# A graph network on one core: parts of edge groups may end in mid-chunk, and gathered rows come in bursts of three chunks

## The chip, the cores and the metric

The kernel runs on 1 core of one Trainium2 chip. The metric is the device time of one execution in microseconds (us). The engines are TensorE (PE, with its weight loads as PEld), VectorE (DVE), ScalarE (ACT), GpSimd (POOL) and SyncE (SP). Each has one stream of instructions, which it works off in the order in which they were written.

## What is computed

There are N = 6250 nodes with 256 features and E = 100,000 edges. The edges are sorted by their target `dst`, and the targets lie denser at low node numbers. Two layers of a graph network sum the rows of the neighbours, each followed by two dense products; at the end come the residual and a layer norm.

```python
def _gin_agg(h, src, dst, eps, n_nodes):
    agg = jax.ops.segment_sum(h[src], dst, num_segments=n_nodes)
    return (1.0 + eps) * h + agg
...
h = _gin_agg(x, src, dst, eps1, n)          # 6250 x 256
h = relu(relu(h @ W1a + b1a) @ W1b + b1b)   # 6250 x 512
h = _gin_agg(h, src, dst, eps2, n)
out = relu(h @ W2a + b2a) @ W2b + b2b       # 6250 x 256
x = _layernorm(x + out)
```

## The kernel before, in words

**Chunks.** The edges are cut into 782 chunks of 128. The first 308 chunks belong to eight crowded tiles of 128 nodes (the "heavy" tiles; seven and 288 chunks in layer 2). Their sums are made by counting edges per pair of nodes and multiplying with whole rows (lines 1734 and 1766 count, 1630 multiplies in layer 1, 1522 in layer 2). All other chunks, 474 in layer 1 and 494 in layer 2, are gathered: for each, GpSimd issues one indirect DMA (line 501) that brings the 128 source rows into SBUF, 256 floats wide in layer 1, 512 in layer 2.

**Groups and parts.** `places` (line 141) packs consecutive chunks into groups of 4h chunks (80 groups; h is 1 to 4). Group by group, the chunks are split into four parts of h chunks. A part may touch at most 32 consecutive nodes, a group at most 128. For each chunk VectorE builds a 128x32 selection matrix (line 1076), and TensorE multiplies it with the gathered rows (line 1127): part b adds into partitions 32b to 32b+31 of a PSUM bank. `members` takes the chunks of a group so that the part changes from one to the next; four chunks in a row thus write to four different strips of 32 partitions. A matmul of float32 shows as two records in the trace.

**Merging.** When the sums of a group are done, ScalarE and VectorE split them in two halves of precision (lines 1157 and 1162), TensorE puts the four parts to their place with two matmuls of a 128x128 matrix `to` (line 1172), and VectorE adds the result into the accumulators of the 1 to 3 node tiles that the group touches (line 1184). In layer 1 two groups share a bank and one turn of splits. When a tile has all its sums, its dense work follows: transposes (line 1234), the first product (line 1273), the second (line 1302); layer 1 writes its rows `h1` to DRAM, which layer 2 gathers.

**Rings.** Gathered rows come in pieces of at most `BURST` = 4 chunks of one group, into a ring of `PIECES` = 6 places. The first gather into a place waits until the sums of the piece that lay there before are done (line 507). Layer 1 sums one piece at a time, layer 2 joins three (`JOIN`).

**What sets the order.** While the program is built, `Plan` (line 293) plays the engines with costs and waits, and writes each engine's instructions in the order that comes out; sums have the first turn on TensorE, merges the second, dense work the third, the products of line 1522 the last. `GATHERS` (us per gather), `LANDINGS` (us until its rows are there), `SUMS` and `TURN` (cost of a piece's matmuls) are such costs. They are not in the program: on the chip an engine takes its stream in this order and waits where data is not there yet. Line 1196 writes matmuls without use where the plan finds TensorE idle late in a layer. The groups are worked off from the highest nodes to the lowest.

Of the kernel before, what the change touches and what calls it, by code (L numbers as in the profile page):

```python
# [17 lines left out]
P = 128  # L18
# [4 lines left out]
BURST = 4  # L23
PIECES = 6
# [116 lines left out]
def places(N, E, c, chunks):  # L141
# [47 lines left out]
GATHERS = (1.28, 1.265)  # L189
LANDINGS = (14.0, 10.0)  # L190
LOAD = 6.0
LANDED = 2.5
SUMS = 0.0021
# [9 lines left out]
BEGAN = 4.5  # L203
# [165 lines left out]
def tile_gin_residual_layernorm(  # L369
# [56 lines left out]
    groups, lo, hi = (a + b for a, b in zip(places(N, E, NC2, NC), places(N, E, NC, NCH)))  # L426
# [4 lines left out]
    NCP = groups[-1][0] + PARTS * groups[-1][1]  # L431
# [43 lines left out]
    members = {}  # L475
# [17 lines left out]
    def gather(number, i, table, width, *places):  # L493

        if i >= len(pieces[number]):
# [9 lines left out]
            for j, (c, b) in enumerate(pieces[number][i][1])  # L505
# [30 lines left out]
    with tc.tile_pool(name="prep", bufs=1) as prep, tc.tile_pool(  # L536
# [10 lines left out]
        assert all(c >= halves * HALF for i in range(EARLY) for c, _ in pieces[1][i][1])  # L547
# [35 lines left out]
        nc.vector.memset(first[0:1, :], 1.0)  # L583
        ones = prep.tile([P, 1], F16, name="ones")
# [32 lines left out]
        for (c, h), top in zip(groups, hi):  # L617
            tops[c : c + PARTS * h] = [top * P + P - 1] * (PARTS * h)
# [80 lines left out]
        def in_groups(g0, g1):  # L699

            c, h = groups[g0]
            return dstf[:, c : c + PARTS * h * (g1 - g0)]

        for g0, g1 in runs:
            h = groups[g0][1]
            nc.tensor.matmul(
                heads[:, PARTS * g0 : PARTS * g1], first,
                in_groups(g0, g1).rearrange("p (g h) -> p g h", h=h)[:, :, 0],
                start=True, stop=True,
            )  # L710
# [12 lines left out]
        compare, add_compare = nc.vector.tensor_tensor, nc.vector.scalar_tensor_tensor  # L723
# [24 lines left out]
        spans = []  # L748
        for g0, g1 in runs:
            c, h = groups[g0]  # L750
            if c + PARTS * h * (g1 - g0) > real:
                g1 -= 1
                spans.append((g1, g1 + 1, (real - groups[g1][0]) // h))
                assert groups[g1][0] + spans[-1][2] * h == real
            if g0 < g1:
                spans.insert(0, (g0, g1, PARTS))

        def beside(do, v, each):

            for g0, g1, parts in spans:  # L760
                c, h = groups[g0]
                n = (PARTS * (g1 - g0 - 1) + parts) * h
                if each:
                    l, f = h, heads[:, PARTS * g0 : PARTS * (g1 - 1) + parts]
                else:
                    l, f = parts * h, bases[:, g0:g1]
                to, of = (
                    a[:, o : o + n].rearrange("p (g l) -> p g l", l=l)
                    for a, o in ((v, c - NC2), (dstf, c))
                )  # L770
                do(to, f.unsqueeze(2).to_broadcast(list(to.shape)), of)

        for each, n in ((True, SLOTS), (False, P)):
            violated(
                lambda v: beside(lambda to, f, d: compare(to, f, d, op=ALU.is_gt), v, each), ng
            )
            violated(
                lambda v: beside(
                    lambda to, f, d: add_compare(
                        to, f, float(n - 1), d, op0=ALU.add, op1=ALU.is_lt  # L780
                    ), v, each,
                ), ng,
            )
# [85 lines left out]
    def ordered(ctx):  # L869
# [13 lines left out]
        def layer(number, ctx, table, width, scale, wa, ba, wb, bias, wide):  # L883
# [177 lines left out]
            def selecting():  # L1061
                for g in order:
# [8 lines left out]
                    sel_token = yield ("get", sel_one if h == 1 else sel_many, 0)  # L1071
# [24 lines left out]
            def sums():  # L1096
# [9 lines left out]
                while i < len(pieces[number]):  # L1106
# [10 lines left out]
                    for i in some:  # L1117
# [7 lines left out]
                        for l, (c, b) in enumerate(pieces[number][i][1]):  # L1125
                            part = [c_ for c_, b_ in members[g] if b_ == b]
                            mm = nc.tensor.matmul(  # L1127
                                pm[b * SLOTS : (b + 1) * SLOTS],
                                sel[:, c - groups[g][0], :], rows_[:, l, :],
                                start=(c == part[0]), stop=(c == part[-1]),  # L1130
                            )
                            if l == 0:
                                together(mm, reads[1:])
                        last_sum[i] = mm
                        fetch_rows(i + PIECES)
                        if i == last[g]:
                            sel_token.used()
                            if g == gs[-1]:
                                plan.then(plan.start, merge([
                                    (k, sels[k][1], SLOTS * len({b for _, b in members[k]}),  # L1140
# [930 lines left out]
```

## Time and profile before

| | us |
|---|---|
| median of three runs (lowest, highest) | 1298.17 (1293.37, 1298.98) |
| the profiled execution | 1295.27 |
| its span, first to last instruction | 1293.5 |
| TensorE busy | 1177.7 (91%) |
| VectorE busy | 876.3 (68%) |
| GpSimd busy (gathers) | 940.9 (73%) |
| ScalarE busy | 555.6 (43%) |

Busy time of GpSimd leaves out the 0.3 us between two gathers that the profile calls "issue". Ends of matmuls are modelled and overlap with the next start, so a cost on TensorE is best read from one start to the next.

### The profile page before, as it was taken

Reading aid. Unit: us, or ns where it says so; the run is one execution under the profiler, and the core shown is the slowest. Engines: PE = TensorE matmul, PEld = TensorE weight load, DVE = VectorE, ACT = ScalarE, POOL = GpSimd, SP = SyncE. Lnnn points to the kernel's source line nnn. Section 1 sums busy time; section 2 is a strip of 40 time slices with the busy share of each in tenths; the row PEclk is TensorE's granted clock in tenths of the full one; section 3 lists DMA queues with packets and bytes.
Section 4 is the critical chain, followed back from the end, with each engine's and each line's share of the span. In section 5 each row is a group of like instructions: output and inputs, shape, how many; then the busy total and the mean of one; then the engine's idle time right before and its main releaser. Section 6 shows DMA issues by size and latency. Waiting matters only on the chain. (4 is left out here: it accounts for less than half of the span.)

```text
span 1293.5 us, 18734 instructions
## 1 busy us (share of the span) xinstructions
PE 1177.7 (91%) x6088; PEld 747.2 (58%) x6088; DVE 876.3 (68%) x2098; ACT 555.6 (43%) x1014; POOL 940.9 (73%) x995
## 2 busy tenths in 40 slices
PE   5689999898998788889888999999999999999987
PEld 3335555554545444554455666767676667776755
DVE  8899889687898898442247867886566656554433
ACT  6335653664245521562454534343343434432221
POOL 7777777777777777777176777777777777777771
PEclk7789999999999999899988999999999999999999
DMA  6755685569546774588299879888898889877782
GB/s 188 216 153 174 213 236 157 186 204 251 153 136 211 194 207 131 163 233 248 79 354 319 284 232 310 266 271 269 288 300 268 288 286 291 290 236 229 236 254 82
DMA packets 190146, 293.86 MB, mean 227 GB/s; under 512 B 67246, under 2 KB 122948, under 8 KB 190040
## 3 DMA queue, kind: packets, MB, share of 16 engines
q0 software_dynamic: 62272, 191.69, 48.0%
q1 hardware_dynamic: 120292, 87.28, 22.4%
q10 hardware_dynamic: 7476, 13.60, 2.9%
q8 instruction: 52, 0.85, 0.3%
q14 instruction: 54, 0.44, 0.1%
HBM read 266.46 MB, written 26.02 MB: 226 GB/s over the span
## 5 line engine op out<-in xcount | busy, mean ns | idle before, releaser
L501 POOL DMA_INDIRECT early<-in_x_dram,srcs x474 | 465.6, 982 | 146.4 <-issue 119.7
L501 POOL DMA_INDIRECT early<-h,srcs x250 | 238.9, 956 | 103.5 <-issue 62.5
L501 POOL DMA_INDIRECT late<-h,srcs x244 | 234.0, 959 | 76.5 <-issue 60.6
L1184 DVE SCALAR_TENSOR_TENSOR acc<-bank,mask,acc 128x512 f32<-128x512 f32 (+1 forms) x374 | 215.6, 608 | 36.9 <-PE bank L1172 35.1
L1127 PE MATMUL bank<-early,sel 128*32 128x256 f32 (+1 forms) x1448 | 140.6, 479 | 52.0 <-DMA early<-in_x_dram,srcs 30.1
L1302 PE MATMUL bank<-wide_w,ht 128*128 128x512 f32 (+1 forms) x392 | 185.4, 597 | 1.6 <-ACT acc L1009 1.5
L1273 PE MATMUL bank<-zt,wide_w 128*128 128x256 f32 (+2 forms) x832 | 180.8, 371 | 3.0 <-ACT zt L1246 3.0
L1273 PEld LDWEIGHTS bank<-zt,wide_w 128*128 128x128 f32 x832 | 150.8, 192 | 33.6 <-ACT zt L1246 5.7
L1522 PE MATMUL bank<-upper,cf 128*128 128x512 f32 (+1 forms) x343 | 152.2, 444 | 5.1 <-ACT upper L1414 4.5
L1522 PE MATMUL bank<-xr,cf 128*128 128x512 f32 (+1 forms) x343 | 138.3, 403 | 2.0 <-DVE xr L1419 2.0
L1076 DVE TENSOR_TENSOR sel<-iota,slot 128x256 f32<-128x256 f32 (+3 forms) x112 | 49.8, 444 | 103.2 <-PE bank L1127 99.2
L1127 PEld LDWEIGHTS bank<-early,sel 128*32 128x32 f32 x1448 | 35.3, 111 | 144.2 <-issue 107.3
L1630 PE MATMUL bank<-xh,cf 128*128 128x512 f32 x392 | 111.9, 428 | 0.3 <-DVE xh L1586 0.3
L1766 DVE TENSOR_TENSOR at<-bank,at 128x490 f32 (+3 forms) x175 | 105.7, 604 | 6.5 <-DVE cb L1696 1.6
L1172 PE MATMUL bank<-split,to 128*128 128x512 f32 (+2 forms) x316 | 89.4, 395 | 21.0 <-DVE split L1162 11.5
L1302 PEld LDWEIGHTS bank<-wide_w,ht 128*128 128x128 f32 (+1 forms) x392 | 69.8, 189 | 62.5 <-issue 55.1
L1302 PE MATMUL bank<-narrow_w,ht 128*128 128x256 f32 (+1 forms) x392 | 102.4, 388 | 2.5 <-ACT ht L1283 2.5
L1157 ACT CAST split<-bank 128x512 fp32r<-128x512 f32 (+2 forms) x121 | 68.8, 577 | 81.7 <-PE bank L1127 77.3
L1162 DVE TENSOR_TENSOR split<-bank,split 128x512 fp32r<-128x512 f32 (+2 forms) x121 | 79.1, 673 | 36.2 <-ACT split L1157 35.7
L1273 PE MATMUL bank<-zt,narrow_w 128*128 128x256 f32 (+2 forms) x432 | 99.2, 375 | 2.3 <-ACT zt L1246 1.6
L1449 ACT CAST cf<-ci 128x512 fp32r<-128x512 uint8 (+3 forms) x91 | 53.7, 592 | 106.7 <-PE bank L1522 86.3
L1696 DVE TENSOR_SCALAR cb<-numbers,spot 128x492 f16<-128x492 f16 (+6 forms) x308 | 85.9, 322 | 19.6 <-PE bank L1734 19.6
(139 smaller groups left out, 1605.7 us busy)
## 6 DMA issues: line engine op xcount, KB each, us to landing
raw<-in_x_dram SPq DMA_DIRECT2D x48, 512.0 KB
h<-h1r ACTq DMA_DIRECT2D x48, 256.0 KB
xr<-h SPq DMA_DIRECT2D x12, 1024.0 KB
acc<-h SPq DMA_DIRECT2D x19, 512.0 KB
early<-in_x_dram,srcs POOLq DMA_INDIRECT x474
r<-in_x_dram SPq DMA_DIRECT2D x22, 256.0 KB
out_dram<-r SPq DMA_DIRECT2D x22, 256.0 KB
acc<-in_x_dram SPq DMA_DIRECT2D x21, 256.0 KB
```

The source lines that it names most:

```text
L501: nc.gpsimd.indirect_dma_start(out=rows_[:, j, :], out_offset=None, in_=table, in_offset=bass.IndirectOffsetOnAxis(ap=srcs[:, c : c + 1], ...
L1127: mm = nc.tensor.matmul(pm[b * SLOTS : (b + 1) * SLOTS], sel[:, c - groups[g][0], :], rows_[:, l, :], start=(c == part[0]), stop=(c == par ...
L1157: nc.scalar.copy(split[:used, 0, i * width : j * width], ap[:used, i * width : j * width])
L1162: nc.vector.tensor_tensor(split[:used, 1, i * width : j * width], ap[:used, i * width : j * width], split[:used, 0, i * width : j * width] ...
L1172: nc.tensor.matmul(pu[:, i * width : (i + 1) * width], to[:used], split[:used, l, i * width : (i + 1) * width], start=(l == 0), stop=(l == 1),
L1184: nc.vector.scalar_tensor_tensor(acc[t], pu[:, i * width : (i + 1) * width], mask[:, t - lo[g], g : g + 1], acc[t], op0=ALU.mult, op1=ALU.add,
L1273: nc.tensor.matmul(ph[:, (f - o) * TILES * P : (f - o) * TILES * P + nb], wa[:, k, f * P : (f + 1) * P], zt[:, k, :nb], start=(k == 0), st ...
L1302: nc.tensor.matmul(po[:m], ht[:, f, i * P : i * P + m], wb[:, f, :], start=(f == 0), stop=(f == KH - 1),)
L1522: nc.tensor.matmul(bank[token.number][:, :width], cf[:m, j, :], of[:m, j, :], start=(j == 0 and of is upper), stop=(j == len(ks) - 1 and o ...
L1630: nc.tensor.matmul(bank[tokens[i].number][:, : 2 * width], cf[:m, j, :], xh[:m, j, :, :].rearrange("p a d -> p (a d)"), start=(k == 0), st ...
L1696: made = nc.vector.tensor_scalar(token.tile[:, :e], numbers[:, :e], spot[:, c : c + 1], None, op0=ALU.is_equal,)
L1766: nc.vector.tensor_tensor(to, bank[token[0].number][:, : NT * w].rearrange("p (k w) -> p k w", w=w), to, op=ALU.add,)
```

## The change

A part may now be a whole number of half chunks long. `places` takes groups of 2 chunks more or less instead of 4 for the 474 chunks beyond the heavy tiles, so h may be 1.5, 2.5 or 3.5. The code gives 60 groups instead of 80 (58 instead of 78 in layer 1): 29 with h = 1.5, 14 with 2.5, 7 with 3.5, 6 with 2, and four others. In the 50 groups with a half, two chunks lie across a border between parts. Each such chunk gets two matmuls with 64 rows, the lower half into one part, the upper half into the next. `BURST` becomes 3 and `PIECES` 8; a piece still ends with its group, so 474 chunks make 172 pieces (before 119), 494 make 180 (before 124), some of them with 1 or 2 chunks. A group with h = 2.5 has pieces of 3, 3, 3 and 1 chunks. The plan's costs change: `LANDINGS` from 14 and 10 to 20 and 12, `SUMS` from 0.0021 to 0.0019, two others by little. Before the layers, the check of the group borders is rewritten and has a few instructions more.

```diff
-BURST = 4
-PIECES = 6
+BURST = 3
+PIECES = 8
...
-            n -= PARTS
-        groups.append((c, n // PARTS))
+            n -= step
+        if n % PARTS and c + n > chunks:
+            n -= n % PARTS
+        groups.append((c, n / PARTS if n % PARTS else n // PARTS))
...
-GATHERS = (1.28, 1.265)
-LANDINGS = (14.0, 10.0)
+GATHERS = (1.285, 1.265)
+LANDINGS = (20.0, 12.0)
...
-SUMS = 0.0021
+SUMS = 0.0019
...
-BEGAN = 4.5
+BEGAN = 5.3
...
+        a + b for a, b in zip(places(N, E, NC2, NC, PARTS), places(N, E, NC, NCH, PARTS // 2))
...
-        members[g] = [
-            (c0 + b * h + i, b) for i in range(h) for b in range(PARTS) if c0 + b * h + i < NCH
-        ]
+        n, l = int(PARTS * h), int(2 * h)
+        ks = sorted(range(n), key=lambda k: (2 * k % l, 2 * k // l))
+        members[g] = [c0 + k for k in ks if c0 + k < NCH]
+        for k in range(n):
+            b, last = 2 * k // l, (2 * k + 1) // l
+            parts_of[c0 + k] = [(b, 0, P)] if b == last else [(b, 0, P // 2), (last, P // 2, P)]
...
-                    sel_token = yield ("get", sel_one if h == 1 else sel_many, 0)
+                    sel_token = yield ("get", sel_one if n <= 2 * PARTS else sel_many, 0)
...
-                        for l, (c, b) in enumerate(pieces[number][i][1]):
-                            part = [c_ for c_, b_ in members[g] if b_ == b]
+                        for k, (l, c, b, p0, p1) in enumerate(some_):
+                            part = [c_ for c_, b_, _, _ in seen if b_ == b]
                             mm = nc.tensor.matmul(
                                 pm[b * SLOTS : (b + 1) * SLOTS],
-                                sel[:, c - groups[g][0], :], rows_[:, l, :],
+                                sel[p0:p1, c - groups[g][0], :], rows_[p0:p1, l, :],
                                 start=(c == part[0]), stop=(c == part[-1]),
                             )
```

In the order of the whole program, the sums' matmuls go from 474 to 574 in layer 1 and from 494 to 594 in layer 2. The merges' go from 156 to 116 and from 160 to 120, VectorE's additions of line 1184 from 186 to 149 and from 188 to 151, the splits on ScalarE and VectorE from 121 to 91 each. The gathers stay 474 and 494. The matmuls without use go from 55 to 35. New line numbers: sums 1149, merges 1194, transposes 1256, first products 1295, second 1324, products with whole rows 1544.

The first place is TensorE's stream in the middle of layer 1, before:

```order
L1127 MATMUL bank_480<-early,sel 32x256 x4
L1734 LDWEIGHTS ca
L1734 MATMUL bank_477<-cb,ca 128x343
L1734 LDWEIGHTS ca
L1734 MATMUL bank_473<-cb,ca 128x343
L1273 MATMUL bank_479<-zt,narrow_w 128x256 x4
L1734 LDWEIGHTS ca
L1734 MATMUL bank_474<-cb,ca 128x343
L1734 LDWEIGHTS ca
L1734 MATMUL bank_477<-cb,ca 128x343
L1302 MATMUL bank_475<-wide_w,ht 128x512 x2
L1127 MATMUL bank_480<-early,sel 32x256 x4
```

and now, in a group with h = 2.5:

```order
L1149 MATMUL bank_491<-early,sel 32x256 x3
L1324 MATMUL bank_493<-wide_w,ht 128x512 x2
L1324 MATMUL bank_496<-wide_w,ht 128x512 x2
L1149 MATMUL bank_491<-early,sel 32x256 x4
L1756 LDWEIGHTS ca
L1756 MATMUL bank_490<-cb,ca 128x441
L1756 LDWEIGHTS ca
L1756 MATMUL bank_490<-cb,ca 128x441
L1149 MATMUL bank_491<-early,sel 32x256 x2
L1652 MATMUL bank_495<-xh,cf 128x512 x4
```

A piece was four matmuls. Now the pieces of this group have 3, 3, 4 and 2: the last two hold the two cut chunks, of which each has two matmuls of 64 rows, and other work stands between the pieces as before.

The second place is TensorE's stream from the last sums of layer 1 on (1302 and 1324 are second products), before:

```order
L1127 MATMUL bank_474<-early,sel 32x256 x4
L1302 MATMUL bank_476<-wide_w,ht 128x512 x2
L1172 MATMUL bank_475<-split,to 128x256 x2
L1302 MATMUL bank_476<-wide_w,ht 128x512 x2
L1234 MATMUL bank_478<-ident,acc 128x128 x2
L1234 MATMUL bank_477<-ident,acc 128x128 x2
L1196 LDWEIGHTS numbers
L1196 MATMUL bank_480<-numbers 128x492
L1273 MATMUL bank_479<-zt,narrow_w 128x128 x4
L1273 MATMUL bank_473<-zt,narrow_w 128x128 x4
L1273 MATMUL bank_474<-zt,narrow_w 128x128 x4
L1273 MATMUL bank_475<-zt,narrow_w 128x128 x4
```

and now:

```order
L1149 MATMUL bank_496<-early,sel 32x256 x4
L1324 MATMUL bank_497<-wide_w,ht 128x512 x2
L1194 MATMUL bank_491<-split,to 128x256 x2
L1295 MATMUL bank_495<-zt,narrow_w 128x128 x4
L1295 MATMUL bank_493<-zt,narrow_w 128x128 x4
L1295 MATMUL bank_494<-zt,narrow_w 128x128 x4
L1295 MATMUL bank_490<-zt,narrow_w 128x128 x4
L1256 MATMUL bank_496<-ident,acc 128x128 x2
L1324 MATMUL bank_497<-wide_w,ht 128x512 x2
L1256 MATMUL bank_491<-ident,acc 128x128 x2
L1324 MATMUL bank_495<-wide_w,ht 128x512 x2
L1324 MATMUL bank_497<-wide_w,ht 128x512 x2
```

Behind the pieces shown there, the layer ends before with 8 more second products, and now with 16 more first products and 10 more second ones. In all, behind its last sums, layer 1 had 16 first products of 128 columns and 12 second products; it now has 32 and 18.

The third place is TensorE's stream at the end of layer 2, before:

```order
L1127 MATMUL bank_6096<-early,sel 32x512 x4
L1302 MATMUL bank_6095<-narrow_w,ht 128x256 x2
L1273 MATMUL bank_6099<-zt,wide_w 128x128 x8
L1127 MATMUL bank_6096<-late,sel 32x512 x4
L1302 MATMUL bank_6095<-narrow_w,ht 128x256 x2
L1302 MATMUL bank_6098<-narrow_w,ht 128x256 x2
L1172 MATMUL bank_6093<-split,to 128x512 x2
L1302 MATMUL bank_6098<-narrow_w,ht 128x256 x2
L1196 LDWEIGHTS numbers
L1196 MATMUL bank_6097<-numbers 128x492
```

and now:

```order
L1544 MATMUL bank_6118<-upper,cf 128x512
L1544 MATMUL bank_6118<-xr,cf 128x512
L1149 MATMUL bank_6112<-early,sel 32x512 x3
L1324 MATMUL bank_6111<-narrow_w,ht 128x256 x2
L1149 MATMUL bank_6112<-early,sel 32x512
L1256 MATMUL bank_6113<-ident,acc 128x128 x4
L1324 MATMUL bank_6111<-narrow_w,ht 128x256 x2
L1295 MATMUL bank_6115<-zt,wide_w 128x128 x8
L1194 MATMUL bank_6114<-split,to 128x512 x2
L1295 MATMUL bank_6116<-zt,wide_w 128x128 x8
L1256 MATMUL bank_6118<-ident,acc 128x128 x4
L1218 LDWEIGHTS numbers
```

Products with whole rows (1544) now stand until right before the last two pieces; before, the last of them (1522) stood where 87% of the sums had been made. Behind the last sums, layer 2 had 16 first products of 128 columns and 10 second products of 256; it now has 32 first products of 128 columns, 16 of 256, and 18 second products.

## Rows read from the trace of the kernel before

**Rows 1.** The page: span, and busy time by engine (share) xinstructions.
```profile
span 1293.5 us, 18734 instructions
PE 1177.7 (91%) x6088; PEld 747.2 (58%) x6088; DVE 876.3 (68%) x2098; ACT 555.6 (43%) x1014; POOL 940.9 (73%) x995
```

**Rows 2.** GpSimd in order of time: start us, us, what [idle before].
```profile
5.26 1.10 POOL L501 DMA_INDIRECT early<-in_x_dram,srcs  x1 [2.29 <-DVE srcs L650]
...
614.03 0.95 POOL L501 DMA_INDIRECT early<-in_x_dram,srcs  x1 [0.30 <-issue]
639.82 1.21 POOL L501 DMA_INDIRECT early<-h,srcs  x1 [24.85 <-DMA h<-h1r]
...
1266.96 0.95 POOL L501 DMA_INDIRECT late<-h,srcs  x1 [0.30 <-issue]
```

**Rows 3.** Waits of GpSimd: us in total, times, longest us.
```profile
POOL early L501 <- PE bank L1127: 6.7, 13, 3.1
...
POOL late L501 <- PE bank L1127: 4.0, 6, 2.3
```

**Rows 4.** Windows: busy us (x) of PE, PEld, DVE, ACT, POOL; clock.
```profile
50.00:600.00 550.00, 491.23 (x2493) 277.65 (x2493) 435.61 (x1036) 264.43 (x468) 419.90 (x428) 0.97 0.65 190
700.00:1250.00 550.00, 538.17 (x2892) 380.75 (x2885) 346.54 (x705) 208.49 (x394) 414.60 (x434) 0.99 0.85 271
```

**Rows 5.** Waits of TensorE, columns as in Rows 3.
```profile
PE bank L1127 <- DMA early<-in_x_dram,srcs: 30.1, 23, 2.9
```

**Rows 6.** Chain that ended last, layer 2: start us, us, what xrecords.
```profile
977.97 3.45 PE bank L1273 x16
...
1062.83 2.71 PE bank L1127 x24
...
1262.63 1.00 PE bank L1127 x8
```

**Rows 7.** TensorE in order of time: merges of both layers.
```profile
473.92 0.82 PE L1172 MATMUL bank<-split,to 128*128 128x256 f32 x4
474.67 0.64 PE L1127 MATMUL bank<-early,sel 128*32 128x256 f32 x8
...
1053.57 1.08 PE L1172 MATMUL bank<-split,to 128*128 128x512 f32 x4
1054.48 0.81 PE L1302 MATMUL bank<-narrow_w,ht 128*128 128x256 f32 x3
```

**Rows 8.** Window of line 1196 alone: PE, PEld, clock.
```profile
1200.00:1290.00 90.00, 6.48 (x21) 2.06 (x21) 0.98 0.65 196
```

**Rows 9.** TensorE in order of time: the end of layer 1.
```profile
619.63 0.64 PE L1127 MATMUL bank<-early,sel 128*32 128x256 f32 x8
620.20 1.98 PE L1302 MATMUL bank<-wide_w,ht 128*128 128x512 f32 x4
...
624.82 3.84 PE L1273 MATMUL bank<-zt,narrow_w 128*128 128x128 f32 x32
628.49 7.03 PE L1302 MATMUL bank<-wide_w,ht 128*128 128x512 f32 x16
635.36 0.37 PE L1196 MATMUL bank<-numbers 128*128 128x492 f16 x1
```

**Rows 10.** TensorE, then VectorE, in order of time: end of layer 2.
```profile
1273.75 1.06 PE L1127 MATMUL bank<-late,sel 128*32 128x512 f32 x8
1274.75 1.99 PE L1302 MATMUL bank<-narrow_w,ht 128*128 128x256 f32 x8
1276.39 0.82 PE L1172 MATMUL bank<-split,to 128*128 128x512 f32 x2
...
1288.21 0.41 DVE L1347 TENSOR_SCALAR r<-r,mv,rs 128x256 f32<-128x256 f32 x1
```

**Rows 11.** VectorE by line and shape: xcount | busy us, mean ns.
```profile
L1184 DVE SCALAR_TENSOR_TENSOR acc<-bank,mask,acc 128x512 f32<-128x512 f32 x188 | 131.1, 741 | 33.0 <-PE bank L1172 31.3
L1184 DVE SCALAR_TENSOR_TENSOR acc<-bank,mask,acc 128x256 f32<-128x256 f32 x186 | 84.4, 473 | 3.9 <-PE bank L1172 3.8
```

More of the change, by code (lines that the diff above doesn't have):

```diff
@@ L138, in bounds, with places @@
     return low, high
-def places(N, E, c, chunks):
+def places(N, E, c, chunks, step):
     def node(e, side):
@@ L425, in tile_gin_residual_layernorm @@
     assert NC2 <= NC and HEAVY[1] <= HEAVY[0]
-    groups, lo, hi = (a + b for a, b in zip(places(N, E, NC2, NC), places(N, E, NC, NCH)))
+    groups, lo, hi = (
+        a + b for a, b in zip(places(N, E, NC2, NC, PARTS), places(N, E, NC, NCH, PARTS // 2))
+    )
     NG = len(groups)
@@ L504, in gather @@
             )
-            for j, (c, b) in enumerate(pieces[number][i][1])
+            for j, c in enumerate(pieces[number][i][1])
         ]
@@ L546, in tile_gin_residual_layernorm @@
         assert 0 < tail <= P and 0 < full - halves * HALF <= tail
-        assert all(c >= halves * HALF for i in range(EARLY) for c, _ in pieces[1][i][1])
+        assert all(c >= halves * HALF for i in range(EARLY) for c in pieces[1][i][1])
         def raw_tail(a, queue, name):
@@ L747, in tile_gin_residual_layernorm, with beside @@
         violated(compare, NC, near, wide_of, op=ALU.is_ge)
-        spans = []
+        def beside(f, to, of, l):
+            to, of = (x.rearrange("p (g l) -> p g l", l=l) for x in (to, of))
+            return to, f.unsqueeze(2).to_broadcast(list(to.shape)), of
+        ahead = [prep.tile([P, ng], F32, name=f"ahead{k}") for k in range(2)]
         for g0, g1 in runs:
             c, h = groups[g0]
[L751 to L783, printed above, removed]
+            if c + int(PARTS * h) * (g1 - g0) > real:
+                todo = [(g0, g1 - 1, PARTS), (g1 - 1, g1, real - groups[g1 - 1][0])]
+                assert h == 1
+            else:
+                todo = [(g0, g1, PARTS)]
@@ new lines, in tile_gin_residual_layernorm @@
+            for g0, g1, parts in todo:
+                if g0 == g1:
+                    continue
+                c = groups[g0][0]
+                n = int((PARTS * (g1 - g0 - 1) + parts) * h)
+                own, base = (a[:, c - NC2 : c - NC2 + n] for a in ahead)
+                of = dstf[:, c : c + n]
+                f = heads[:, PARTS * g0 : PARTS * (g1 - 1) + parts]
+                compare(*beside(bases[:, g0:g1], base, of, int(parts * h)), op=ALU.subtract)
+                if h == int(h):
+                    compare(*beside(f, own, of, h), op=ALU.subtract)
+                    continue
+                l = int(2 * h)
+                to, of = (x.rearrange("p (q l) -> p q l", l=l) for x in (own, of))
+                f = f.rearrange("p (q t) -> p q t", t=2)
+                for p0, cut in ((0, l // 2 + 1), (P // 2, l // 2)):
+                    some = slice(p0, p0 + P // 2)
+                    for t, js in enumerate((slice(0, cut), slice(cut, l))):
+                        t_ = f[some, :, t : t + 1].to_broadcast([P // 2, n // l, js.stop - js.start])
+                        compare(to[some, :, js], t_, of[some, :, js], op=ALU.subtract)
```

42 lines of the change are left out of this document (30 added, 12 removed).

## The prediction

> **What bounds the kernel now.** I read the page first: TensorE is busy for 91% of the span, GpSimd for 73% [rows 1]. A busy share says little of a kernel of two unlike layers, so next comes GpSimd in order of time. Its first gather starts at 5.26 us and the last of layer 1 at 614.03; the first of layer 2 starts at 639.82 and the last of all at 1266.96 [rows 2]. That is 473 steps of 1.287 us and 493 of 1.272 us, practically without a break. The waits agree: only 6.7 + 4.0 us of GpSimd's time went to sums whose place in the ring was still taken [rows 3]. So the span is a chain of five pieces: 5.3 us of start, 474 gathers (609.7), 24.9 us until the rows of layer 1 are in DRAM, 494 gathers (628.1), and 25.6 us from the last gather to the end. The change leaves the number of gathers as it is; it can move only the two stretches in which GpSimd has nothing to do, and the waits of the ring.
>
> Then TensorE by windows: from 50 to 600 us it is idle for 550 - 491.2 = 58.8 us, from 700 to 1250 us for 550 - 538.2 = 11.8 us [rows 4]. Of the idle time in layer 1, 30.1 us were spent before a sum whose rows had not landed [rows 5]. So layer 1 has some room on TensorE, layer 2 nearly none: there two engines run at the same pace, and whoever gets more work sets the end.
>
> **The sums, step by step.** In layer 2, a joined run of 24 records (12 chunks) takes 2.71 us and a lone piece of 8 records (4 chunks) takes 1.00 [rows 6]. So four chunks that go to the four strips run side by side and take (2.71 - 1.00) / 2 = 0.855 us; I call this a turn. A run costs 0.145 us besides. In layer 1, with half the columns, a lone piece takes 620.20 - 619.63 = 0.57 us [rows 9], which I split in a turn of 0.43 and 0.14 besides. A turn holds four chunks only if they go to four different strips, and a piece with other work behind it ends its turn even when it holds fewer.
>
> Layer 1 sums piece by piece. Before, 119 pieces made 119 turns. Now a group with h = 1.5 (6 chunks) makes one piece of three whole chunks and one of a whole chunk and two cut ones. In the latter one strip gets two matmuls, so it takes two turns: 3 in all. h = 2.5 gives 1 + 1 + 2 + 1 = 5 turns, h = 3.5 gives 5, h = 2 gives 3, the group of h = 3 gives 4, the last one 1. Sum: 29 x 3 + 14 x 5 + 7 x 5 + 6 x 3 + 4 + 1 = 215 turns in 172 pieces. By price: 215 x 0.43 + 172 x 0.14 = 116.5 us against 119 x 0.57 = 67.8, so 48.7 us more.
>
> Layer 2 joins three pieces, which packs better. Three groups of h = 1.5 take 7 turns instead of 4.5, three of 2.5 take 12 instead of 7.5, three of 3.5 take 15 instead of 10.5. Counted over the whole stream it is 181 turns in 64 runs against 124 in 44: 57 x 0.855 + 20 x 0.145 = 51.6 us more.
>
> No row shows two matmuls of 64 rows beside each other. From below, four halves take one turn like four whole chunks (they go to four strips); this is my value, since the whole chunks of [rows 6] are the nearest rows. From above, the change from 128 to 64 rows and back costs each time what entering a run costs: it happens inside a piece 43 times in layer 1 and 80 times in layer 2, which adds 6.0 and 11.6 us. The Trainium skill's page on TensorEngine Tiling (Array Packing), section Key Properties, says that a change of tiling mode drains the engine; the 0.145 us beside each run here fits such a drain between 128x128 and 128x32. By that rule the sum would go to its upper end.
>
> **The merges and VectorE.** Twenty groups fewer in each layer. Merges of two groups take 474.67 - 473.92 = 0.75 us in layer 1 and 1054.48 - 1053.57 = 0.91 in layer 2 [rows 7]. So TensorE saves 20 x 0.375 = 7.5 us and 20 x 0.455 = 9.1 us. VectorE saves 37 additions of 473 ns and 37 of 741 ns, together 44.9 us [rows 11], and the splits go down too. I cost all of VectorE's saving at nothing: it has 550 - 435.6 = 114 us of idle time in the window of layer 1 and 203 us in that of layer 2 [rows 4], and no gather waits for it.
>
> Net on TensorE: 48.7 - 7.5 = 41.2 us more in layer 1, 51.6 - 9.1 = 42.5 us more in layer 2.
>
> **What of it is on the path in layer 1.** 41 us go into 58.8 us of idle time, much of which was waiting for rows. That hides most of it, barely. But what the order leaves for after the last sum is exposed. Before, from that sum's start to the end of the dense work, TensorE ran without idle time from 619.63 to 635.36 us [rows 9]. Now 6 second products and 16 first ones more stand there. A second product takes (635.36 - 628.49) / 8 = 0.86 us and a first one (628.49 - 624.82) / 16 = 0.23 [rows 9]: 5.2 + 3.7 = 8.9 us. The rings add some waiting. With pieces of 3, 3, 3 and 1 chunks, 8 places hold 20 chunks instead of 24, so a place is wanted again after 20 x 1.287 = 25.7 us instead of 30.9. The plan expected rows 14 us after a gather, and TensorE still came up to 2.9 us too early [rows 5]; with 3.9 us for the piece itself about 21 of the 25.7 us are gone before a sum can start. TensorE may then lag by 5 us and no more. I put the waits of the ring at 3 us, between 0 and 10. Layer 1: 12 us longer.
>
> **What of it is on the path in layer 2.** 42.5 us meet 11.8 us of idle time and 6.5 us of matmuls without use, which give way [rows 8]. The rest, 24.2 us, has no cover. The order says where it shows: 16 first products of 256 columns at 3.45 / 8 = 0.43 us [rows 6], 16 of 128 columns at 0.23, and 8 second products at (1276.39 - 1274.75) / 4 = 0.41 [rows 10] stand behind the last sum in addition, 13.9 us. The other 10 us come as waits of GpSimd for the ring, since TensorE falls behind. What ends the kernel is the same as now, a last second product and a layer norm [rows 10].
>
> **The small parts.** A few more checks and two memsets run on VectorE before the layers, while GpSimd already gathers its first ring; nothing. The later `LANDINGS` alone only move sums behind other work; their price is in the ring and in the two ends. The granted clock is 0.97 and 0.99 in the two windows [rows 4], so nearly all of them is at 2.4 GHz and little at 1.2; a fuller stream can win at most these 1 to 3% of TensorE's time there, and I count nothing.
>
> **Sum.** 1295.3 us of the profiled execution + 12 + 24 = 1331 us. That execution lies 2.9 us under the median of the runs (1298.2), so I predict 1334 us. Below, all times are such medians.
>
> **Rivals.**
> - Only the ends grow: TensorE's other work packs tighter than I think and all the rest hides. Then 8.9 + 13.9 = 23 us remain, 1321 us; with half of the added work at the ends hidden as well, 1310. For it: the 58.8 idle us of layer 1. Against it: [rows 4] for layer 2.
> - Full price: each change of 64 and 128 rows costs 0.145 us, the ring stops GpSimd in layer 1 (10 us), and the idle time in layer 2 stays idle, since it is waiting for ScalarE and VectorE: 8.9 + 10 + 6 + 42.5 + 11.6 = 79 us, 1377 us.
> - The halves run one after the other, four turns instead of one in each of the 50 groups: 50 x 3 x (0.43 + 0.855) = 193 us of TensorE more than in the forecast, with no cover left, 1527 us. The Trainium skill, TensorEngine Tiling (Array Packing), section Gotcha 1, has a rule for this: different row tiles can't access the same PSUM bank at once, and the halves do share a bank. No run here shows it. Against it: the four strips of one bank run side by side in [rows 6].
> - Faster: TensorE binds layer 2, and a cut chunk costs no more than a whole one, so that sums cost as before per chunk. Then the merges' 9.1 us come off layer 2 and some 3 us off the end of layer 1, 1286 us. It decides if short pieces overlap with the work behind them. Against it: a lone piece of layer 1 takes 0.57 us to the next start, with nothing beside it.
> - Nothing changes: GpSimd sets the pace and TensorE's addition hides in both layers and at both ends, 1298 us. The products behind the last sums speak against it.
>
> **How the numbers follow.** Forecast 55% (own range 1320 to 1350), only the ends 15% (1305 to 1322), full price 10% (1350 to 1380), halves in series 5%, nothing changes 8%, faster 7%. Slower by over 0.5% (6.5 us, about what a measurement of this kernel can tell from no change): 55 + 15 + 10 + 5 = 85%; within 8%; faster 7%. The range from 1300 to 1380 leaves out the halves in series, the faster case and most of the unchanged one, 18%.
>
> **What would show it.** Right: a lone piece of layer 1 at 0.57 us with three or four matmuls and about 1.0 with a whole chunk and two cut ones; TensorE's idle time from 50 to 600 us under 25 us; about 25 us from the last sum of layer 1 to its last second product; in layer 2 TensorE without a break and GpSimd's waits for sums well above 10.7 us; over 30 us from the last gather to the end. Wrong: gathers that run through as now and both ends no longer than now (nothing changes, or faster), or a piece with two cut chunks that takes over 2 us in layer 1 (series). If single steps of the gathers became shorter than 1.27 us, the chain above would have a part that I take as fixed.

## The result and the profile after

The changed kernel takes 1342.86 us in the median (1339.23 to 1347.94, 6 runs), the kernel before on the same chip 1296.93 (1293.37 to 1298.98, 6 runs). The ratio is 1.0358, with a 95% interval from 1.0337 to 1.0379: 3.6% slower. The forecast was 1334 us in a range from 1300 to 1380.

The page of the profile first, as in [rows 1]. TensorE went from 91% to 95% of a longer span, VectorE and GpSimd fell.

```profile
span 1337.2 us, 19154 instructions
PE 1266.4 (95%) x6400; PEld 739.0 (55%) x6400; DVE 827.6 (62%) x2013; ACT 539.8 (40%) x984; POOL 936.1 (70%) x995
```

GpSimd in order of time answers to [rows 2] (start us, us, what, idle before): first and last gather of layer 1, first of layer 2, last of all.

```profile
5.74 1.10 POOL L509 DMA_INDIRECT early<-in_x_dram,srcs  x1 [2.76 <-DVE srcs L662]
...
612.31 0.95 POOL L509 DMA_INDIRECT early<-in_x_dram,srcs  x1 [0.30 <-issue]
646.49 0.98 POOL L509 DMA_INDIRECT early<-h,srcs  x1 [33.23 <-DMA h<-h1r]
...
1289.13 0.95 POOL L509 DMA_INDIRECT early<-h,srcs  x1 [0.30 <-issue]
```

From it the chain in its five pieces: start 5.7 us (before 5.3), gathers of layer 1 607.5 (609.7), turn to layer 2 33.2 (24.8), gathers of layer 2 643.6 (628.1), tail 47.1 (25.6). The 43.7 us of the span are +0.4, -2.2, +8.4, +15.5 and +21.5. All but 6.6 of them lie in layer 2 and its tail.

GpSimd's waits for a place in the ring, which were 6.7 and 4.0 in [rows 3] (us in total, times, longest):

```profile
POOL early L509 <- PE bank L1149: 19.7, 36, 2.7
POOL late L509 <- PE bank L1149: 17.9, 12, 3.7
```

Counting only what each such wait has above the 0.30 us that any gather stands before its start, layer 1 has none and layer 2 has 23.1 us (before 5.0).

TensorE in the two windows of [rows 4] (length, then busy us and instructions of PE, PEld, DVE, ACT, POOL; granted clock; busy share and GB/s of the DMA engines): its idle time in layer 1 fell from 58.8 to 23.0 us, in layer 2 from 11.8 to 9.8 only.

```profile
50.00:600.00 550.00, 526.98 (x2633) 273.67 (x2636) 422.21 (x1003) 258.06 (x455) 419.00 (x431) 0.98 0.67 194
700.00:1250.00 550.00, 540.20 (x2809) 345.36 (x2808) 297.21 (x604) 191.69 (x357) 399.07 (x421) 0.99 0.83 263
```

The view that turned out most useful cuts the run in two at the first gather of layer 2: layer 1 with its turn, and layer 2 with its tail. The changed kernel:

```profile
5.74:646.50 640.76, 599.70 (x2958) 311.69 (x2956) 463.58 (x1160) 298.34 (x525) 463.43 (x475) 0.98 0.64 186
646.50:1337.20 690.70, 665.88 (x3440) 426.46 (x3440) 359.90 (x740) 239.25 (x456) 470.39 (x494) 0.99 0.79 252
```

The kernel before, cut in the same way:

```profile
5.26:639.80 634.54, 554.60 (x2789) 311.79 (x2787) 480.06 (x1195) 303.72 (x535) 465.62 (x474) 0.95 0.64 188
639.80:1293.50 653.70, 622.32 (x3297) 434.56 (x3297) 392.49 (x793) 249.61 (x476) 472.94 (x494) 0.98 0.83 266
```

In the first half TensorE has 45.1 us more to do and the half is 6.2 us longer: the rest went into idle time (79.9 us before, 41.1 after). In the second it has 43.6 us more, and the half is 37.0 us longer: there was little idle time to go into (31.4 before, 24.8 after).

Where the added work comes from shows in TensorE's order of time in layer 1 (start, us, what, records). A piece of one whole and two cut chunks (10 records) takes 77.45 - 76.33 = 1.12 us to the next start, a piece of three whole chunks (6 records) 81.64 - 81.08 = 0.56, as much as four whole ones before, 0.57 in [rows 9].

```profile
76.33 1.19 PE L1149 MATMUL bank<-early,sel 128*32 128x256 f32 x10
77.45 3.70 PE L1324 MATMUL bank<-wide_w,ht 128*128 128x512 f32 x8
81.08 0.63 PE L1149 MATMUL bank<-early,sel 128*32 128x256 f32 x6
81.64 0.59 PE L1756 MATMUL bank<-cb,ca 128*128 128x490 f16 x2
```

The end of layer 1, which answers to [rows 9], in the same columns. The last sum consists of four halves of 64 rows (8 records) and starts at 618.09 us; the last second product is through at 642.03, 23.9 us later (before 15.7).

```profile
618.09 0.64 PE L1149 MATMUL bank<-early,sel 64*32 64x256 f32 x8
618.66 1.98 PE L1324 MATMUL bank<-wide_w,ht 128*128 128x512 f32 x4
...
635.16 7.03 PE L1324 MATMUL bank<-wide_w,ht 128*128 128x512 f32 x16
642.03 0.37 PE L1218 MATMUL bank<-numbers 128*128 128x492 f16 x1
```

The end of layer 2, which answers to [rows 10]. Whole-row products still stand between the last sums; the last sum starts 12.8 us after the last gather has ended at 1290.08 (before 5.8 us), and from its start to the end of the span are 34.3 us (before 19.8).

```profile
1300.51 0.39 PE L1544 MATMUL bank<-xr,cf 128*128 128x512 f32 x1
1300.83 1.06 PE L1149 MATMUL bank<-early,sel 128*32 128x512 f32 x6
1301.82 1.13 PE L1324 MATMUL bank<-narrow_w,ht 128*128 128x256 f32 x4
1302.88 1.04 PE L1149 MATMUL bank<-early,sel 128*32 128x512 f32 x2
...
1323.99 4.48 PE L1324 MATMUL bank<-narrow_w,ht 128*128 128x256 f32 x20
```

### The profile page after: what moved, and what is told of

Its sections match the earlier page's. It is cut to its first block, busy times and chain, and to the rows that moved or that the text cites. A ratio compares the mean times of both kernels' runs of the same rounds, so it can differ in the third digit from the quotient of the medians.

```text
span 1337.2 us, 19154 instructions
## 1 busy us (share of the span) xinstructions
PE 1266.4 (95%) x6400; PEld 739.0 (55%) x6400; DVE 827.6 (62%) x2013; ACT 539.8 (40%) x984; POOL 936.1 (70%) x995
## 5 line engine op out<-in xcount | busy, mean ns | idle before, releaser
L509 POOL DMA_INDIRECT late<-h,srcs x241 | 230.1, 955 | 87.6 <-issue 57.0
L1149 PE MATMUL bank<-early,sel 128*32 128x256 f32 (+3 forms) x1754 | 240.1, 469 | 2.0 <-DMA early<-in_x_dram,srcs 1.9
L1206 DVE SCALAR_TENSOR_TENSOR acc<-bank,mask,acc 128x256 f32<-128x256 f32 (+1 forms) x300 | 174.1, 608 | 51.9 <-PE bank L1194 51.2
L1149 PEld LDWEIGHTS bank<-early,sel 128*32 128x32 f32 (+1 forms) x1754 | 50.1, 108 | 158.9 <-issue 140.0
L1487 DVE TENSOR_TENSOR acc<-bank,acc 128x512 f32<-128x512 f32 x84 | 57.6, 686 | 96.4 <-PE bank L1544 96.3
L1652 PE MATMUL bank<-xh,cf 128*128 128x512 f32 x392 | 105.6, 409 | 0.0
L1149 PE MATMUL bank<-late,sel 128*32 128x512 f32 (+1 forms) x582 | 102.4, 601 | 0.0
L1093 DVE TENSOR_TENSOR sel<-iota,slot 128x192 f32<-128x192 f32 (+6 forms) x118 | 50.6, 429 | 81.8 <-PE bank L1149 76.0
L1179 ACT CAST split<-bank 128x512 fp32r<-128x512 f32 (+2 forms) x91 | 51.9, 574 | 110.8 <-PE bank L1149 109.0
```

The lines of the kernel that those rows point to most:

```text
L509: nc.gpsimd.indirect_dma_start(out=rows_[:, j, :], out_offset=None, in_=table, in_offset=bass.IndirectOffsetOnAxis(ap=srcs[:, c : c + 1], ...
L1149: mm = nc.tensor.matmul(pm[b * SLOTS : (b + 1) * SLOTS], sel[p0:p1, c - groups[g][0], :], rows_[p0:p1, l, :], start=(c == part[0]), stop=( ...
L1179: nc.scalar.copy(split[:used, 0, i * width : j * width], ap[:used, i * width : j * width])
L1206: nc.vector.scalar_tensor_tensor(acc[t], pu[:, i * width : (i + 1) * width], mask[:, t - lo[g], g : g + 1], acc[t], op0=ALU.mult, op1=ALU.add,
L1487: nc.vector.tensor_tensor(acc[t], bank[token.number][:, :width], acc[t], op=ALU.add)
L1652: nc.tensor.matmul(bank[tokens[i].number][:, : 2 * width], cf[:m, j, :], xh[:m, j, :, :].rearrange("p a d -> p (a d)"), start=(k == 0), st ...
```

## The experiments

My theory, T: pieces of three chunks and cut chunks load TensorE with some 45 us per layer; in layer 1 that is hidden, in layer 2 it binds. Its rival, R: the load would fit, and the ring or the plan's costs hold the gathers back. In the table "half 2" is layer 2 with its tail; busy and idle are TensorE's there; the ring waits are GpSimd's above 0.30 us each, as far as the profile puts them down to the sums' line. With those that it puts down to other lines of TensorE or to a DMA, layer 1 has 35.9 in "whole parts" and 24.0 in "bursts of four". Times but the medians are from one profiled execution each, in us. The changed kernel was not timed again beside the edits: the kernel before took 1297.33 us on the chip of the first four and 1295.81 us on that of the others, and each ratio is to the kernel before on the same chip.

| kernel | median | ratio to before | gathers 1 | turn | gathers 2 | tail | half 2 | busy | idle | ring 1 / 2 |
|---|---|---|---|---|---|---|---|---|---|---|
| before | 1296.93 | 1 | 609.7 | 24.8 | 628.1 | 25.6 | 653.7 | 622.3 | 31.4 | 0 / 5.0 |
| changed | 1342.86 | 1.0358 | 607.5 | 33.2 | 643.6 | 47.1 | 690.7 | 665.9 | 24.8 | 0 / 23.1 |
| one matmul | 1328.88 | 1.0237 | 609.5 | 33.2 | 632.4 | 45.9 | 678.3 | 643.9 | 34.4 | 0 / 8.5 |
| 128 rows | 1336.92 | 1.0306 | 604.7 | 33.0 | 645.4 | 46.3 | 691.7 | 660.7 | 31.0 | 0 / 20.4 |
| no lower | 1312.08 | 1.0132 | 604.9 | 33.0 | 625.1 | 37.7 | 662.8 | 606.3 | 56.5 | 0 / 0.8 |
| whole parts | 1367.92 | 1.0571 | 643.6 | 21.2 | 671.3 | 22.6 | 693.9 | 652.5 | 41.4 | 28.9 / 49.7 |
| SUMS 0.0016 | 1334.59 | 1.0277 | 608.8 | 28.9 | 655.1 | 35.2 | 690.3 | 670.2 | 20.1 | 0 / 31.2 |
| costs of before | 1362.64 | 1.0507 | 610.1 | 51.4 | 622.1 | 68.7 | 690.8 | 665.9 | 24.9 | 0 / 0 |
| bursts of four | 1395.59 | 1.0752 | 631.1 | 20.8 | 711.3 | 22.7 | 734.0 | 676.3 | 57.7 | 19.1 / 87.7 |
| before, new costs | 1320.97 | 1.0181 | 611.2 | 22.9 | 654.5 | 22.8 | 677.3 | 628.6 | 48.7 | 0 / 29.6 |

**On another chip first.** The edits "one matmul", "128 rows", "whole parts" and "no lower" ran first on a chip on which the kernel before itself took 1593.67 us. They came out at 1.0125 [1.0038, 1.0212], 1.0114 [1.0029, 1.0200], 1.0507 [1.0441, 1.0573] and 1.0173 [1.0098, 1.0248] of that. The waits are longer there (TensorE waited 22.9 us for one check on VectorE in "one matmul", 2.3 here), while the gathers of layer 1 themselves take the same time (465.3 and 465.4 us in "one matmul"). Why, I can't say, so nothing about the forecast is taken from them. What follows are the runs of the same edits on the chip where the kernel before took 1297.33 us.

**One matmul for a cut chunk.** Each cut chunk goes whole, with one matmul of 128 rows, to the first of its two parts; the sums over its other part are left out.

```diff
-            parts_of[c0 + k] = [(b, 0, P)] if b == last else [(b, 0, P // 2), (last, P // 2, P)]
+            parts_of[c0 + k] = [(b, 0, P)]
```

> The same kernel as one_matmul (each cut chunk in one matmul of 128 rows, output not the reference's), timed again where the kernel before takes about 1297 us. T: 24.6 us of TensorE less in layer 1, hidden, and 29.6 us less in layer 2, of which GpSimd's waits and the late last sum give back 20 to 28 us: 1315 to 1323 us. Rival R (ring and later expected rows): waits for sums stay at about 38 us, 1337 to 1343 us.

1328.88 us, ratio 1.0237 [1.0196, 1.0277]. Half 2 of this kernel:

```profile
648.50:1326.80 678.30, 643.92 (x3240) 432.75 (x3240) 358.99 (x740) 238.95 (x456) 472.11 (x494) 0.97 0.80 257
```

TensorE's busy time there is 22.0 us shorter, but that is not the whole price of the second matmuls. The sums' line alone, in the changed kernel and in this one (half 2; length, then busy us and records of that line, granted clock, DMA):

```profile
646.50:1337.20 690.70, 179.40 (x1188) 0.99 0.79 252
648.50:1326.80 678.30, 150.93 (x988) 0.97 0.80 257
```

That is 28.5 us less; T had 29.6. The rest of TensorE's work took longer because more of half 2 ran at the lower clock: by the trace's records of the granted clock 42.0 us were at 1.2 GHz, with TensorE busy in 27.8 of them, in the changed kernel 18.0 us, with 13.6 busy. What that level costs shows in the kernel before, where a joined run of 24 records at a granted clock of 0.50 takes 704.31 - 699.03 = 5.28 us to the next start, and 2.71 at 2.4 GHz [rows 6]:

```profile
699.03 5.35 PE L1127 MATMUL bank<-early,sel 128*32 128x512 f32 x24 [4.25 <-ACT zt L1246]
704.31 3.55 PE L1273 MATMUL bank<-zt,wide_w 128*128 128x234 f32 x16
```

Of the 37.0 us that half 2 had grown by, 12.4 are gone; TensorE is idle 9.6 us longer. Another 21.6 us of its busy time over the kernel before, net of fewer merges and matmuls without use, remain with pieces of three. The result lies between both expected ranges: T's direction, with a little more than half its size.

**Two matmuls of 128 rows.** Both matmuls of a cut chunk take all 128 rows, so no run changes its rows. The two parts get rows of each other.

```diff
-            parts_of[c0 + k] = [(b, 0, P)] if b == last else [(b, 0, P // 2), (last, P // 2, P)]
+            parts_of[c0 + k] = [(b, 0, P)] if b == last else [(b, 0, P), (last, 0, P)]
```

> The same kernel as rows128 (both matmuls of a cut chunk with 128 rows, output not the reference's), timed again. T with 0.14 us for each change of rows: 1328 to 1335 us. If the change of rows is free: 1340 to 1345 us.

1336.92 us, ratio 1.0306 [1.0268, 1.0344], whose interval overlaps the changed kernel's; the time lies between the two expected ranges, in neither. On the engine the change of rows has a price. The sums' line, in the same columns as above: half 1 of the changed kernel and of this one, then half 2 of this one and of the kernel before (line 1127).

```profile
5.74:646.50 640.76, 134.96 (x1148) 0.98 0.64 186
5.74:643.50 637.76, 129.95 (x1148) 0.97 0.64 187
643.50:1335.20 691.70, 167.83 (x1188) 0.97 0.78 252
639.80:1293.50 653.70, 119.33 (x988) 0.98 0.83 266
```

So the changes of rows cost 5.0 us in layer 1 and 179.40 - 167.83 = 11.6 us in layer 2. In the changed kernel's chain (start, us, what, records) runs of equal length show it: 18 records take 2.69 us without a change, 2.83 with one (10 records of 128 rows, then 8 of 64) and 2.96 with two, about 0.14 for each change.

```profile
991.24 2.96 PE bank L1149 x18
1000.26 2.83 PE bank L1149 x18
...
1160.58 2.69 PE bank L1149 x18
```

Half 2 did not become shorter, though (691.7 against 690.7). TensorE's whole busy time there fell by 5.2 us only, because 36.1 us of this half ran at 1.2 GHz (27.5 of them busy) where the changed kernel had 18.0 (13.6), and its idle time grew by 6.2. What the change of rows is worth on the path at a like clock is not settled by this run.

**Without half of the whole-row products.** The products with the matrix of low halves (`xr`) in line 1544 are left out: a load taken off layer 2 that has nothing to do with sums or the ring.

```diff
-                                for of in (upper, xr):
+                                for of in (upper,):
```

> The same kernel as no_lower (without the second half of precision of the products with whole rows in layer 2), timed again. T: 79 us of TensorE go from layer 2, GpSimd's waits for sums there fall under 11 us, and the longer ends of both layers (8 + 15 us) stay: 1316 to 1324 us, no less. Rival R: waits over 30 us, 1335 to 1343 us.

1312.08 us, ratio 1.0132 [1.0088, 1.0175]: 4 us under T's range, which was to end there ("no less"). TensorE is busy for 59.6 us less in half 2 (56.8 us of it ran at 1.2 GHz, after 18.0, so the 79 us of T do not show in full), and half 2 is 27.9 us shorter; the ring waits of layer 2 are gone, 0.8 us after 23.1, with the ring and the plan's costs untouched. That GpSimd waits in the changed kernel because TensorE is late is shown by this; R has no reason for it. T's two ends came (turn 8.2 and tail 12.1 us longer than before, 8 and 15 expected); the time lies lower because the gathers of the two layers were 4.8 and 3.0 us shorter than before, which T did not have. A larger ring with pieces of three was not tried, so how much the shorter ring adds to the waits stays open. Below that GpSimd itself ends layer 2: 625.1 us of gathers, 622.1 in the run where it never waits ("costs of before").

**Groups of whole parts again.** The 80 groups of before, with bursts of three and the new costs.

```diff
-        a + b for a, b in zip(places(N, E, NC2, NC, PARTS), places(N, E, NC, NCH, PARTS // 2))
+        a + b for a, b in zip(places(N, E, NC2, NC, PARTS), places(N, E, NC, NCH, PARTS))
```

> The same kernel as whole_parts (80 groups of whole chunks, pieces of three, the new plan costs), timed again. T: short pieces cost TensorE as much as cut chunks: 1312 to 1332 us. If the cut chunks are the whole cause: 1295 to 1302 us. Rival R: 1335 us or more.

1367.92 us, ratio 1.0571 [1.0518, 1.0623], slower than the changed kernel. T missed. A group of four chunks becomes pieces of 3 and 1, and eight such pieces hold 16 chunks; the ring stops GpSimd for 28.9 us in layer 1 (35.9 with the waits put down to other lines, which is what its gathers there are longer by) and 49.7 in layer 2. For this kernel R's mechanism is the right one. So bursts of three can't be judged alone: with groups of four chunks they leave the ring short, with groups of six, which the cut chunks bring, less so.

**Another price for a sum's column.** Only the plan's order changes: with `SUMS` at 0.0016 it puts less behind the last sums.

```diff
-SUMS = 0.0019
+SUMS = 0.0016
```

> The changed kernel with the plan's price of a sum's column at 0.0016 in place of 0.0019, nothing else; behind the last sums stand 12 second products in layer 1 (18 in the changed kernel, with 24 in place of 32 first ones) and 6 in layer 2 (18, with 16 in place of 48 first ones, and no whole-row products). T (the two ends are long because of what the plan leaves behind the last sums, and TensorE's load of 60 us more binds layer 2 whatever the order): the turn falls from 33.2 to 25 to 28 us, the tail from 47.1 to 30 to 38 us, what left the ends comes back in part as GpSimd's waits in layer 2, 1315 to 1332 us. Rival (it is all the plan's order, the load fits in TensorE's idle time): 1295 to 1310 us. Second rival (the ends wait for rows, not for the order): 1338 to 1348 us, turn and tail as in the changed kernel.

1334.59 us, ratio 1.0277 [1.0219, 1.0335]. The two halves:

```profile
5.75:643.50 637.75, 598.82 (x2964) 311.67 (x2962) 464.65 (x1160) 299.55 (x525) 464.61 (x475) 0.98 0.64 187
643.50:1333.80 690.30, 670.17 (x3458) 428.00 (x3458) 357.97 (x740) 240.65 (x456) 472.78 (x494) 0.98 0.79 252
```

The tail is 11.9 us shorter, the gathers of layer 2 are 11.5 longer; half 2 stays at 690.3 us. What I had split into "behind the last sum" and "waits for the ring" is one quantity, which this order only moved. That is no rule for every order: with the old groups the new costs made half 2 longer by 23.6 us (last experiment). The turn did get 4.3 us shorter. 1334.59 is a little above T's range of 1315 to 1332, since I had expected the ends to win more than the waits take back.

**The costs of before with the new groups.**

```diff
-GATHERS = (1.285, 1.265)
-LANDINGS = (20.0, 12.0)
+GATHERS = (1.28, 1.265)
+LANDINGS = (14.0, 10.0)
-SUMS = 0.0019
+SUMS = 0.0021
-BEGAN = 5.3
+BEGAN = 4.5
```

> The changed kernel's 62 groups and bursts of three with the plan's costs of the kernel before (rows after 14 and 10 us, 0.0021 a column of a sum, groups 1.28 us, 4.5 us at the start). Behind the last sums stand 32 second products in layer 1 in place of 18, and in layer 2 36 in place of 18 with 32 whole-row products in place of 16 transposes. T (what stands behind the last sums sets both ends): the turn grows from 33.2 to 42 to 50 us, the tail from 47.1 to 60 to 80 us, GpSimd's waits in the layers fall by 5 to 25 us, 1347 to 1385 us. Rival (later expected rows are what costs time, since products are then held back that could have run early): 1310 to 1335 us. No weight in the costs: 1338 to 1347 us.

1362.64 us, ratio 1.0507 [1.0447, 1.0567], inside T's range, with the turn (51.4) a little above its step and the tail (68.7) inside it. (The new groups are 60 in number, not 62 as the expectations for this run and the next have it.) The halves:

```profile
5.75:667.20 661.45, 604.74 (x2961) 314.82 (x2959) 466.56 (x1160) 298.85 (x525) 465.94 (x474) 0.97 0.62 180
667.20:1358.00 690.80, 665.91 (x3445) 425.49 (x3445) 359.50 (x740) 239.77 (x456) 471.80 (x494) 0.99 0.78 252
```

And the longest of TensorE's waits (us in total, times, longest):

```profile
PE bank L1149 <- DMA early<-in_x_dram,srcs: 28.0, 25, 4.3
```

Half 2 is again 690.8 us, now with a tail of 68.7 and no ring waits at all. The whole difference to the changed kernel, 20.7 us, lies in half 1: TensorE waits 28.0 us there for rows that the plan expected 14 us after the gather, and 1.9 us where it expects them after 20. What it did not do in that time stands behind the last sum, and the turn takes 51.4 us. So T's reason holds for the turn only: the longer tail cost nothing, since the ring waits went for it. The new costs are a gain of the change, with its groups. That it is the later rows among the four is what the waits speak for; `LANDINGS` alone was not tried.

**Bursts of four with the new groups.**

```diff
-BURST = 3
-PIECES = 8
+BURST = 4
+PIECES = 6
```

> The changed kernel with bursts of four chunks and a ring of six pieces, as before; the 62 groups with their cut chunks and the new costs stay. A piece can hold all four parts again, so that by the price of a turn the sums take some 82 us of TensorE in layer 1 (123 in the changed kernel) and 146 in layer 2 (177); 8 second products stand behind the last sum of layer 1 and 4 behind that of layer 2. T (the turns of the short pieces are what loads TensorE): PE's busy time falls by 50 to 80 us, turn 21 to 26, tail 22 to 30, GpSimd's waits under 12 us in each layer, 1285 to 1308 us. Rival (the ring is what counts: groups of six chunks leave a ring of 18 chunks in place of 24, so that GpSimd waits for places): waits of 15 to 45 us in each layer, 1312 to 1360 us.

1395.59 us, ratio 1.0752 [1.0692, 1.0812]: slower than either range. Six chunks are pieces of 4 and 2, the ring holds 18 chunks, and GpSimd stops once for each six pieces, from 724 to 951 us every 28 us or so (start, us, what, idle before):

```profile
808.62 0.94 POOL L509 DMA_INDIRECT late<-h,srcs  x1 [5.76 <-PE bank L1149]
...
836.84 0.94 POOL L509 DMA_INDIRECT late<-h,srcs  x1 [5.78 <-PE bank L1149]
```

TensorE is idle for 57.7 us of half 2. The sums do pack better, 152.92 us on their line in half 2 after 179.40:

```profile
657.60:1391.60 734.00, 152.92 (x1188) 0.96 0.76 237
```

TensorE's busy time there grew all the same, by 43.4 us of matmuls without use (141), after 8.3 (26) in the changed kernel, and by the clock: 59.1 us of this half were at 1.2 GHz, after 18.0. R's mechanism, and more than its size; T's gain is there on the engine and not in the time.

**The new costs with the kernel before.** The converse: `GATHERS`, `LANDINGS`, `SUMS` and `BEGAN` of the change, with 80 groups and bursts of four.

```diff
...
-LANDINGS = (14.0, 10.0)
+LANDINGS = (20.0, 12.0)
...
```

> The kernel before, with its 80 groups and bursts of four, with the plan's new costs alone (rows after 20 and 12 us, 0.0019 a column of a sum, groups 1.285 us, 5.3 us at the start). Behind the last sums stand 8 second products in layer 1 (12 wider ones before) and 4 in layer 2 (10 before). T (the costs order the ends, the cut chunks and bursts load TensorE): turn 21 to 25 us, tail 21 to 25 us, the gathers as before, 1288 to 1298 us. Rival (costs that make the plan hold work back cost the time of the changed kernel): 1305 to 1340 us.

1320.97 us, ratio 1.0181 [1.0136, 1.0227]. Turn and tail came as T says (22.9 and 22.8), but 29.6 us of ring waits take their place, which only the rival's time covers. Two of these waits have 7.2 us each. Here is the first, on TensorE and then on GpSimd:

```profile
840.35 1.11 PE L1234 MATMUL bank<-ident,acc 128*128 128x128 f32 x4 [5.21 <-DVE acc L1184]
841.25 1.91 PE L1302 MATMUL bank<-narrow_w,ht 128*128 128x256 f32 x4
842.96 1.06 PE L1234 MATMUL bank<-ident,acc 128*128 128x128 f32 x4
843.95 3.50 PE L1127 MATMUL bank<-late,sel 128*32 128x512 f32 x24
...
846.04 1.01 POOL L501 DMA_INDIRECT late<-h,srcs  x1 [7.20 <-PE bank L1127]
```

TensorE stands 5.21 us before transposes whose sums VectorE has not added up; the joined run of 24 records, which would free the ring, is behind them in its order. Which of the four costs makes that order was not tried.

No kernel of these beats the kernel before. Of those with the new groups, `SUMS` at 0.0016 is the fastest that computes everything.

## Why the prediction was right, and which term was too small

By pieces, the profiled execution was forecast as 1295.3 + 12 + 24 and took 1339.23 = 1295.3 + 43.9. The mechanism held: layer 1 hid most of TensorE's added work, layer 2 had little room for it. That the total is off by 8 us only is in part luck, since layer 1 came out 5 us under its term and layer 2 13 us over. Of the signs named beforehand one did not come: TensorE had breaks in layer 2 still (9.8 us in the window, 11.8 before).

- **Layer 1: 12 us forecast, 6.6 measured.** The products behind the last sum were put at 8.9 us; the turn grew by 8.4. TensorE's work was put 41.2 us higher and its busy time was 45.1 higher, and as forecast most of it went into idle time. The work itself grew by more, about 56 us (an estimate): 61.4 us of half 1 were at 1.2 GHz before (45.4 of them busy), 30.7 after (23.5), which gave back some 11 us that the forecast had put at nothing. Of the difference to 41.2, 5.0 us are changes of rows. The 3 us for the ring did not come: no wait above 0.30 us there. The gathers were 2.2 us shorter, less than they differ between the variants without ring waits (604.7 to 611.2).
- **Layer 2: 24 us forecast, 37.0 measured.** This is the mis-sized term, and the part of it that failed is the change of 64 and 128 rows: I took it at nothing ("this is my value") and kept 11.6 us as upper bound. It costs 11.6 us, by the sums' line of "128 rows". The turns were counted about right: without the changes the sums take 167.83 - 119.33 = 48.5 us more than before (51.6 forecast). The matmuls without use were right as well: 14.5 us before, 8.3 after, 6.2 less (6.5 forecast). Two smaller terms were off in opposite ways. I let all 11.8 idle us of the window vanish, where half 2 lost 6.6 of its 31.4: of the 24.8 left, 18.3 are waits for ScalarE's and VectorE's results, which the added work did not fill. And I counted nothing for the clock, which gave back about 7.3 us: 32.6 us of half 2 were at 1.2 GHz before (28.2 busy), 18.0 after (13.6), and work at that level takes about twice as long (5.28 against 2.71 us above). So the work, at a like clock, is an estimated 43.6 + 7.3 = 50.9 us more, not 42.5 - 6.5 = 36.0, and 14.9 - 7.3 + 5.2 are the 12.8 us between forecast and measurement. Of the rival "full price", the price of each change and, in the main, the idle time that stays came true; its ring waits in layer 1 did not.
- **Where it shows.** I had it as 13.9 us behind the last sum and 10 as ring waits. From the last sum to the end it is 14.6 us more; the gathers took 15.5 more, and the last sum itself came 7.0 us later behind the last gather. The runs with other costs show that with these groups the split is the plan's choice: half 2 was 690.7, 690.3 and 690.8 us with tails of 47.1, 35.2 and 68.7.
- **The halves side by side.** They do run as four strips: four halves took 618.66 - 618.09 = 0.57 us, as much as four whole chunks. The rival with halves in series is out. The rule of the Trainium skill, TensorEngine Tiling (Array Packing), Gotcha 1, is out with it as a price for this kernel: halves of different rows into different strips of one bank show no delay here. The same page of the Trainium skill says in its section Key Properties that a change of tiling mode drains the engine. The trace agrees, with about 0.14 us for each change in the chain, and the sum did go to the upper end in this term.
- **The later rows** I had costed at nothing of their own. With the new groups the four new costs together are worth 20 us (1362.64 to 1342.86), by which the forecast already went, since it was made from the changed order; with the old groups they cost 24.

The 24.6 us of half 2 that "one matmul" leaves are, by the table, 21.6 us of TensorE's busy time and 3.0 us of idle time, at nearly the same clock (28.2 us busy at 1.2 GHz before, 27.8 in "one matmul"); the sums' line alone has 150.93 - 119.33 = 31.6 us more, and fewer merges and matmuls without use take some off. Not settled: what pieces of three, which fill a turn to three quarters, cost in time by themselves. Both kernels that were to tell it ran into the ring.

## What to carry to other kernels

Where two engines run at one pace, count the busy and idle time of the fuller one over the whole stage with its tail, not in a window without its ends: an order can move the loss between waits and tail, and a look at either alone reads as a gain. Before two busy times are compared, look at the granted clock of both stretches, or compare the line that was changed: here the price of the changes of rows was 11.6 us on their line and 5.2 in the engine's total. Fewer, fuller groups did not pay here where the pieces that feed them left a strip or the ring unfilled: look at group size, piece size and ring together. A plan's costs belong to one layout; when the layout changes, run old and new costs with both.

## What the hardware showed

- Four matmuls of 64 rows into four strips of one bank take what four of 128 rows take (0.57 us in layer 1), but mixing them in a run costs about 0.14 us at each change (18 records: 2.69, 2.83, 2.96 us).
- Three strips cost as much as four: 0.56 us for three chunks and 0.57 for four in layer 1.
- The same run of 24 records took 2.71 us at 2.4 GHz and 5.28 us at 1.2 GHz.
